# Attention, routing and eight experts in one hand-ordered kernel: the first query copy in two parts, and one more empty place ahead of the transposes of the normed tokens

## The chip, the cores and the metric

The kernel runs on one core of one Trainium2 chip. The metric is device time in microseconds (us); lower is better. The engines are named as in the profile: PE (TensorE; PEld is its weight load), DVE (VectorE), ACT (ScalarE), POOL (GpSimd), and SP (SyncE), which issues most of the DMAs. Times are of the whole program.

## The reference, cut

```python
def attention_block(x, g, b):             # x: 4 batches, 512 tokens, 128 wide
    xn = layernorm(x, g1, b1)             # x itself is normed once before
    q, k, v = xn @ Wq, *split(xn @ Wkv)   # 16 heads of 64 for q; one k and one v for all heads
    attn = softmax(q * 64**-0.5 @ k.T)
    return layernorm((attn @ v) @ Wo, g2, b2)

x = x + attention_block(layernorm(x))
h = layernorm(x)                          # "hn" in the kernel
probs = softmax(h @ gate_w.T)             # 8 experts
topw, sel = top_k(probs, 2); topw /= topw.sum()
for each expert e: out_e = (up * gelu(gate)) @ down_e   # 128 -> 2 x 512 -> 128
x = x + sum over the two chosen experts of topw * out_e
```

Everything is float32.

## The kernel before, in words

**Layout.** The 2048 tokens are four batches of 512; a batch is held as 128 partitions by 4 token tiles of 128. The 16 heads are 8 pairs. The attention works in *steps*: one step is one head pair and one token tile of one batch, so a batch has 32 steps and there are 128. The experts work in 39 tiles of 128 slots: each token's normed row is scattered to two slots in DRAM, sorted by expert, and a tile loads 128 slots of one expert.

**PSUM.** The pool `ps_sc` holds two score tiles of two banks each, `ps_av` one bank for the values' product, and `ps_tp` three banks that everything else takes in turn: transposes, projections, routing, the experts' transposes and down projections. A tile in `ps_tp` has to be copied out before the third one after it may start.

**The attention loop** (`attention`) is an order written out by hand; each engine runs its own instructions in the order in which the program issues them. One turn of the loop takes two steps, i and i+1:

1. `divide` of step i-1 (L330 to L332), then `score` of i and i+1: matmuls L307 on PE, the row maximum `nmax` L314 on DVE.
2. `pieces(PE)`: a place at which other work may put one piece on PE. If there was none, the turn is called `bare`.
3. `turn` of steps i-5 and i-4: 16 transposes L340 of the weights `ex`, and four copies of the results out of PSUM. In a bare turn ACT copies both halves of the first step (L454, L456) and DVE the first half of the second (L452); otherwise DVE copies the second half of the first step (L456) and ACT the rest (L454, L464). Between them `softmax` (L322, exponentials on ACT).
4. `pieces(REST, SOON)`, two rows of values (L350), `divide` of step i, and `pieces(REST, SOON)` again. In the last batch one more `pieces(SOON)`.

**The other work** is a set of Python generators. A `yield` ends a piece and names the kind of place that the next piece waits for: `PE`, `REST` (a plain `yield`) or `SOON`. `advance` gives one place to the first generator in the queue whose kind fits. The list `aheads` holds `project` of the next batch (norm, transposes L255, keys L278, queries L289 with their copy L291, values L297). The list `others` holds, for the batch that has ended, `output` (L374), then `between` (norm, residual, norm again into `hn` with four ACT instructions L216, then a PE place in which `turned` transposes `hn`, L542, and copies it to `hT`, L544), then `route`: gate matmul L576, `logits` L579, the top-2 choice on DVE (L583 to L604), counts `cp` L625 on PE, slot numbers, eight scatters of `hn` on POOL (L652), and `plan`, which tells which expert each tile is of. `between` runs for batches 0, 1 and 2 beside the attention of the next batch.

**The last batch** has no attention after it, so `between_late` and `route` run beside the experts' tiles (3 places in each tile: in the middle of the up projections L820, behind them, and behind the down projections L833). There `hn` is made by DVE (L529), and `hT` is copied by DVE. An expert tile is: transpose `tp_e` L799 of the next tile, its copy `xeT` L801 on ACT, 16 matmuls `gu` L820, `ge` L825 on ACT, `act` L826 on DVE, 8 matmuls `dn` L833, `ye` L838 on DVE, a scatter of the result on POOL (L850). SP loads the tokens `xt` (L779) and the weights (L786, L789) of the tiles ahead.

**The start** (batch 0): `project(0)` runs alone until the keys and the first query tile are there. `wq` is applied to the normed tokens (L289), ACT copies the 512 columns of the result and scales them (L291), and the first turn's scores begin. The score of step (b, p, t) reads only columns t*128 to t*128+127 of `qT[p]`, and all of `kT`.

Of the kernel before, what the change touches and what calls it, by code (L numbers as in the profile page):

```python
# [19 lines left out]
SCALE = DH ** (-0.5)  # L20
# [12 lines left out]
def tile_attention_then_moe(  # L33
# [15 lines left out]
    nc = tc.nc  # L49
    P = 128  # L50
    B, S, D = x.shape
# [132 lines left out]
    def moments(src, tag, twice=False, st=None):  # L184

        n = src.shape[1]
        if st is None:
            st = small.tile([P, n, 6], F32, tag="st", name=f"st_{tag}")  # L190
            for c in range(n):
                nc.vector.bn_stats(st[:, c, :], src[:, c, :])
            yield
        mv = small.tile([P, n, 2], F32, tag="mv", name=f"mv_{tag}")
        for c in range(n):
            nc.vector.bn_aggr(mv[:, c, :], st[:, c, :])
        ve = small.tile([P, n], F32, tag="ve", name=f"ve_{tag}")
        if twice:
            nc.vector.tensor_scalar(ve, mv[:, :, 1], 1.0 + EPS, EPS * EPS, ALU.mult, ALU.add)
        else:  # L200
            nc.vector.tensor_scalar_add(ve, mv[:, :, 1], EPS)
        rstd = small.tile([P, n], F32, tag="rstd", name=f"rstd_{tag}")
        nc.gpsimd.tensor_tensor(rstd, ve, neg_half[:, 0:n], ALU.pow)
        return mv, rstd

    def normalize(dst, src, tag, twice=False):

        mv, rstd = yield from moments(src, tag, twice)
        n = src.shape[1]

        less = small.tile([P, n], F32, tag="less", name=f"less_{tag}")
        nc.gpsimd.tensor_tensor(less, mv[:, :, 0], rstd, ALU.mult)
        nc.gpsimd.tensor_scalar_mul(less, less, -1.0)
        yield
        for c in range(n):
            nc.scalar.activation(  # L216
                dst[:, c, :], src[:, c, :], AF.Identity, bias=less[:, c : c + 1],
                scale=rstd[:, c : c + 1],
            )

    def pause(n):

        for _ in range(n):
            yield
# [19 lines left out]
    def project(b):  # L244


        xn = p2.tile([P, NT, D], F32, tag="ln", name=f"xn_{b}")
        xnT = p1.tile([P, NT, P], F32, tag="xnT", name=f"xnT_{b}")
        xnT_flat = xnT.rearrange("p c t -> p (c t)")
        if b > 0:  # L250
            yield from normalize(xn, xs[b], f"a{b}", twice=True)
            yield PE
            tp = ps_tp.tile([P, NT, P], F32, tag="tp", name=f"tp_x_{b}")
            for c in range(NT):
                nc.tensor.transpose(tp[:, c, :], xn[:, c, :], ident)  # L255
            nc.scalar.activation(xnT, tp, AF.Identity, bias=b1_sb, scale=g1_sb)
        else:

            mv, rstd = yield from moments(xs[b], f"a{b}", True)
            for c in range(NT):  # L260
                nc.vector.tensor_scalar(
                    xn[:, c, :], xs[b][:, c, :], mv[:, c, 0:1], rstd[:, c : c + 1],
                    ALU.subtract, ALU.mult,
                )
            for h in range(2):
                half = slice(h * NT // 2, (h + 1) * NT // 2)
                tp = ps_tp.tile([P, NT // 2, P], F32, tag="tp", name=f"tp_x_{b}_{h}")
                for c in range(NT // 2):
                    nc.tensor.transpose(tp[:, c, :], xn[:, half][:, c, :], ident)
                if h == 0:  # L270
                    nc.vector.tensor_scalar(xnT[:, half], tp, g1_sb, b1_sb, ALU.mult, ALU.add)
                else:
                    nc.scalar.activation(
                        xnT[:, half], tp, AF.Identity, bias=b1_sb, scale=g1_sb
                    )
        yield PE
        kp = ps_tp.tile([P, S], F32, tag="tp", name=f"kp_{b}")
        nc.tensor.matmul(kp, wkk.rearrange("p j d -> p (j d)"), xnT_flat, start=True, stop=True)  # L278
        kT = p2.tile([P, S], F32, tag="kT", name=f"kT_{b}")

        moved = nc.scalar.copy if b > 0 else nc.vector.tensor_copy
        moved(kT, kp)
        v = p2.tile([P, NT, DH], F32, tag="v", name=f"v_{b}")
        qT = []
        if b > 0:
            yield PE
        for c in range(NP):
            qp = ps_tp.tile([P, S], F32, tag="tp", name=f"qp_{b}_{c}")
            nc.tensor.matmul(qp, wq_sb[:, c, :], xnT_flat, start=True, stop=True)  # L289
            qT.append(p9.tile([P, S], F32, tag="qT", name=f"qT_{b}_{c}"))  # L290
            nc.scalar.mul(qT[c], qp, SCALE)  # L291
            qkv[b] = qT, kT, v
            yield PE
            if c == 0:
                vp = ps_tp.tile([P, NT, DH], F32, tag="tp", name=f"vp_{b}")
                for t in range(NT):
                    nc.tensor.matmul(vp[:, t, :], xnT[:, t, :], wv, start=True, stop=True)  # L297
                moved(v, vp)
                yield PE
# [103 lines left out]
    def attention():  # L403
# [10 lines left out]
        held, exTs, oTs, rows, aheads = {}, {}, {}, [], []  # L414
        tiles = experts()
        aheads.append([project(0), REST])
        while 0 not in qkv:
            advance(aheads)
# [11 lines left out]
        for i in range(0, end + TURN, 2):  # L430
            if 0 < i <= end:
                divide(*steps[i - 1], *held[i - 1])
            if i % (NP * NT) == 10 and steps[i][0] + 1 < B:
                b = steps[i][0] + 1
                aheads.append([project(b), REST])
# [55 lines left out]
    def between(g, y):  # L491


        yn = p2.tile([P, NT, D], F32, tag="ln2", name=f"yn_{g}")
        yield from normalize(yn, y, f"c{g}")
        yield
        nc.gpsimd.tensor_tensor(yn, yn, g2_sb.unsqueeze(1).to_broadcast([P, NT, D]), ALU.mult)
        yield
        nc.gpsimd.tensor_tensor(xs[g], xs[g], yn, ALU.add)
        yield  # L500
        hn = p2.tile([P, NT, ROW], F32, tag="hn", name=f"hn_{g}")
        yield from normalize(hn[:, :, 0:D], xs[g], f"d{g}")
        yield PE
        hs[g] = hn, turned(g, hn)
        yield PE

    def between_late(g, y, st):


        mv, rstd = yield from moments(y, f"c{g}", st=st)  # L510
        yield
        xg = xs[g]
        yn = p2.tile([P, NT, D], F32, tag="ln2", name=f"yn_{g}")
        for c in range(NT):
            nc.vector.scalar_tensor_tensor(
                yn[:, c, :], y[:, c, :], mv[:, c, 0:1], g2_sb, ALU.subtract, ALU.mult
            )
        yield
        yield from pause(1)
        for c in range(NT):  # L520
            nc.vector.scalar_tensor_tensor(
                xg[:, c, :], yn[:, c, :], rstd[:, c : c + 1], xg[:, c, :], ALU.mult, ALU.add
            )
        yield
        hn = p2.tile([P, NT, ROW], F32, tag="hn", name=f"hn_{g}")
        mv, rstd = yield from moments(xg, f"d{g}")
        yield from pause(2)
        for c in range(NT):
            nc.vector.tensor_scalar(  # L529
                hn[:, c, 0:D], xg[:, c, :], mv[:, c, 0:1], rstd[:, c : c + 1],  # L530
                ALU.subtract, ALU.mult,
            )
        yield from pause(1)
        yield PE
        hs[g] = hn, turned(g, hn)
        yield from pause(1)
        yield PE

    def turned(g, hn):
        tp = ps_tp.tile([P, NT, P], F32, tag="tp", name=f"tp_h_{g}")  # L540
        for c in range(NT):
            nc.tensor.transpose(tp[:, c, :], hn[:, c, 0:D], ident)  # L542
        hT = p1.tile([P, NT, P], F32, tag="hT", name=f"hT_{g}")
        (nc.vector.tensor_copy if g == B - 1 else nc.scalar.copy)(hT, tp)  # L544
        return hT
# [407 lines left out]
```

## Time and profile before

| | us |
|---|---|
| median of 3 runs | 582.54 (582.27 to 583.16) |
| the profiled execution | 583.46 |
| its span | 581.7 |
| PE busy | 554.7 (95%) |
| DVE busy | 383.3 (66%) |
| ACT busy | 358.7 (62%) |
| POOL busy | 335.1 (58%) |
| PE's mean granted clock | 0.987 |

The profile shows one execution; its span runs from the first to the last instruction, and the profiled execution's own time is 1.76 us longer. In a timeline line the columns are: start, duration, engine, line of the kernel, instruction, output <- input, the shapes, how many instructions are drawn together (x4), and in brackets the time for which the engine stood idle before it and what ended that. Durations of a group that was drawn together run from the first start to the last end. In the list of waits each row gives the waiting engine and line, the releasing engine and line, the total in us, how often, and the longest. A few matmul records can be missing, so a group may show fewer than were issued.

The attention of batches 0 to 2 fills about 14 to 405 us, that of batch 3 ends at 452, and the experts' tiles fill 458 to 562. In the attention one turn of the loop takes 5.71 us without extra PE work.

### The profile page before, as it was taken

How to read it: one execution, taken by the hardware profiler on the slowest of the kernel's cores; microseconds unless marked ns; L12 is line 12 of the kernel's file. 1: busy time of each engine (PE TensorE's matmuls, PEld its weight loads, DVE VectorE, ACT ScalarE, POOL GpSimd, SP SyncE). 2: the span in 40 equal slices, each digit the busy share in tenths (PEclk: the TensorE clock that was granted, in tenths of full speed). 3: DMA queues.
4: the chain of work that ended last, by engine and by line, in shares of the span. 5: the costliest groups of instructions: out<-in, count | busy, mean ns of one | idle time of the engine just before them, and what ended most of it. 6: DMA issues, size and time to landing. Idle time of an engine off the chain costs nothing.

```text
span 581.7 us, 10509 instructions
## 1 busy us (share of the span) xinstructions
PE 554.7 (95%) x3391; PEld 346.2 (60%) x3391; DVE 383.3 (66%) x949; ACT 358.7 (62%) x912; POOL 335.1 (58%) x354
## 2 busy tenths in 40 slices
PE   7899999999999999999999999999999999999980
PEld 5354455545655545566455546654554999999970
DVE  3767666667668688666677877567795378444433
ACT  2779767776678767867887776678865322222210
POOL 3756554456557568755665787457678045743340
PEclk9999999999999999999999999999999999999995
DMA  8990000000000000200000005000000179999945
GB/s 242 300 279 2 1 1 1 1 1 2 1 1 1 0 2 26 73 5 2 0 1 2 10 22 186 4 2 2 0 7 32 47 231 298 350 339 314 320 139 217
DMA packets 38729, 50.33 MB, mean 87 GB/s; under 512 B 4356, under 2 KB 27142, under 8 KB 38673
## 3 DMA queue, kind: packets, MB, share of 16 engines
q1 hardware_dynamic: 35232, 43.44, 24.2%
q0 software_dynamic: 2144, 4.46, 2.1%
q10 hardware_dynamic: 1296, 1.74, 0.8%
q8 instruction: 28, 0.46, 0.3%
q14 instruction: 29, 0.23, 0.1%
HBM read 37.11 MB, written 15.29 MB: 90 GB/s over the span
## 4 chain that ended last, share of the span: by engine, by line
PE 74%; DVE 6%; issue 5%; ACT 5%; DMA 4%; POOL 4%; SPq 0%; POOLq 0%; DVEq 0%; ACTq 0%
PE av L350 18%; PE sc L307 18%; PE tp L340 18%; PE yp L374 5%; PE qp L289 5%; PE gu L820 4%; DMA parts<-ye,row 3%; ACT ex L322 3%; POOL parts L850 3%; DVE nmax L314 2%; PE dn L833 2%; DMA yy<-parts 1%; PE warm L128 1%; DVE ex L332 1%; PE kp L278 1%
## 5 line engine op out<-in xcount | busy, mean ns | idle before, releaser
L331 POOL TENSOR_SCALAR ex<-ex,rden 128x512 f32<-128x512 f32 x128 | 220.2, 1723 | 143.6 <-DVE rden L330 135.4
L322 ACT ACTIVATE ex<-sc,nmax 128x512 f32<-128x512 f32 x256 | 175.8, 707 | 5.9 <-DVE nmax L314 5.9
L314 DVE TENSOR_REDUCE nmax<-sc 128x2 f32<-128x1024 f32 x128 | 150.1, 1213 | 2.0 <-PE sc L307 2.0
L340 PEld LDWEIGHTS tp<-ident,ex 128*128 128x128 f32 x1024 | 112.9, 141 | 34.8 <-issue 20.9
L307 PE MATMUL sc<-kT,qT 64*128 64x512 f32 x512 | 128.4, 617 | 4.2 <-ACT ex L322 3.5
L340 PE MATMUL tp<-ident,ex 128*128 128x128 f32 x1024 | 128.0, 275 | 0.7 <-ACT exT L454 0.3
L350 PE MATMUL av<-exT,v 128*64 128x512 f32 x512 | 124.9, 605 | 0.2 <-ACT exT L454 0.2
L307 PEld LDWEIGHTS sc<-kT,qT 64*128 64x128 f32 x512 | 43.4, 185 | 87.7 <-ACT ex L322 41.9
L454 ACT COPY exT<-tp 128x512 f32<-128x512 f32 x113 | 66.8, 591 | 19.4 <-PE tp L340 19.2
L330 DVE RECIPROCAL rden<-den 128x2 f32<-128x2 f32 x128 | 21.0, 164 | 83.2 <-ACT ex L322 79.6
L332 DVE TENSOR_SCALAR ex<-ex,rden 128x512 f32<-128x512 f32 x128 | 69.6, 543 | 4.5
L820 PE MATMUL gu<-xeT,gu 128*128 128x128 f32 x560 | 71.1, 281 | 0.0
L825 ACT ACTIVATE ge<-gu 128x512 f32<-128x512 f32 x35 | 20.9, 597 | 73.3 <-PE gu L820 71.0
L820 PEld LDWEIGHTS gu<-xeT,gu 128*128 128x128 f32 x560 | 65.1, 192 | 1.0
L850 POOL DMA_INDIRECT parts<-ye,row x35 | 34.4, 982 | 50.3 <-DVE ye L838 39.9
L350 PEld LDWEIGHTS av<-exT,v 128*64 128x64 f32 x512 | 32.9, 136 | 47.4 <-issue 45.5
L322 ACT ACTIVATION_READ_ACCUMULATOR ex<-sc,nmax 128x1 f32 x256 | 57.0, 223 | 0.0
L826 DVE TENSOR_TENSOR act<-ge,gu 128x512 f32<-128x512 f32 x35 | 24.0, 687 | 41.1 <-ACT ge L825 39.4
L456 DVE COPY exT<-tp 128x512 f32<-128x512 f32 x48 | 33.1, 690 | 26.1 <-PE tp L340 25.8
L291 ACT ACTIVATE qT<-qp 128x512 f32<-128x512 f32 x32 | 19.0, 601 | 38.7 <-PE qp L289 38.7
L464 ACT COPY exT<-tp 128x512 f32<-128x512 f32 x64 | 39.6, 619 | 0.6 <-PE tp L340 0.6
L652 POOL DMA_INDIRECT slots<-hn,index x32 | 33.1, 1036 | 10.9 <-PE tp_e L799 5.9
(160 smaller groups left out, 468.9 us busy)
## 6 DMA issues: line engine op xcount, KB each, us to landing
gu<-in_gate_up_t_dram SPq DMA_DIRECT2D x38, 512.0 KB
down<-in_down_t_dram SPq DMA_DIRECT2D x38, 256.0 KB
slots<-blank SPq DMA_DIRECT2D x26, 360.0 KB
xt<-slots SPq DMA_DIRECT2D x38, 72.0 KB
yy<-parts SPq DMA_DIRECT2D x4, 512.0 KB
out_dram<-x ACTq DMA_DIRECT2D x4, 256.0 KB
x<-in_x_dram SPq DMA_DIRECT2D x3, 256.0 KB
parts<-ye,row POOLq DMA_INDIRECT x35, 4.9
```

The costliest lines, as they stand in the source:

```text
L307: nc.tensor.matmul(sc[:, j, :], qT[p][half, t * P : (t + 1) * P], kT[half, :], start=True, stop=True)
L314: nc.vector.tensor_reduce(nmax, sc, AX.X, ALU.max, negate=True)
L322: nc.scalar.activation(ex[:, j, :], sc[:, j, :], AF.Exp, bias=nmax[:, j : j + 1], accum_out=den[:, j : j + 1],)
L331: nc.gpsimd.tensor_scalar_mul(ex[:, 0, :], ex[:, 0, :], rden[:, 0:1])
L332: nc.vector.tensor_scalar_mul(ex[:, 1, :], ex[:, 1, :], rden[:, 1:2])
L340: nc.tensor.transpose(tp[:, c, :], ex[:, j, c * P : (c + 1) * P], ident)
L350: nc.tensor.matmul(av[j * DH : (j + 1) * DH, :], v[:, c, :], exT[:, j, c, :], start=(c == 0), stop=(c == NT - 1),)
L454: nc.scalar.copy(*copies[0])
L456: (nc.scalar.copy if bare else nc.vector.tensor_copy)(*copies[1])
L464: nc.scalar.copy(*copies[1])
L820: latest[:] = [nc.tensor.matmul(ps[:, j, g, :], gu[:, at : at + P], xT, start=True, stop=True)]
L850: apart(added, nc.gpsimd.indirect_dma_start(parts, bass.IndirectOffsetOnAxis(ap=row[:, c : c + 1], axis=0), y[:, c, :], None, bounds_check ...
```

## The change

Three edits:

- `project`: the very first copy of a query tile (batch 0, head pair 0) is made by two ACT instructions, columns 0 to 127 and columns 128 to 511, instead of one.
- `between` (batches 0, 1, 2): one more plain `yield` behind the norm and ahead of the PE place. `turned`, and all of `route` behind it, come one turn of the loop later.
- `between_late` (batch 3): `pause(2)` instead of `pause(1)` ahead of the PE place: one more of the experts' places is left empty.

```diff
@@ project
             qT.append(p9.tile([P, S], F32, tag="qT", name=f"qT_{b}_{c}"))
-            nc.scalar.mul(qT[c], qp, SCALE)
+
+            for some_of in ([slice(0, P), slice(P, S)] if b == c == 0 else [slice(0, S)]):
+                nc.scalar.mul(qT[c][:, some_of], qp[:, some_of], SCALE)
             qkv[b] = qT, kT, v
             yield PE
@@ between
         hn = p2.tile([P, NT, ROW], F32, tag="hn", name=f"hn_{g}")
         yield from normalize(hn[:, :, 0:D], xs[g], f"d{g}")
+        yield
         yield PE
         hs[g] = hn, turned(g, hn)
         yield PE
@@ between_late
                 ALU.subtract, ALU.mult,
             )
-        yield from pause(1)
+        yield from pause(2)
         yield PE
         hs[g] = hn, turned(g, hn)
         yield from pause(1)
         yield PE
```

How the instructions move on the engines, as the two programs stand: ACT has one instruction more. In batches 0 and 1 `tp_h` and `hT`, and `lp`, `cp` and their ACT and DVE work, stand one turn later. In batch 2, whose turns have no projection of a next batch beside them, the turn that held `tp_h` becomes a bare one and the turn after it does not: ACT and DVE change places in two copies of each. In the last batch `tp_h` stands behind `tp_e` of tile 4 and the down projections of tile 2, instead of ahead of them, and `hT` on DVE behind `ye` of tile 2; the order of SP's instructions is the same.

## The prediction

> **What bounds the kernel now.** I read the page's rows of busy time and of 40 slices first, then the chain of work that ended last, then PE's waits, then the timeline around each edited line.
>
> ```profile
> PE 554.7 (95%) x3391; PEld 346.2 (60%) x3391; DVE 383.3 (66%) x949; ACT 358.7 (62%) x912; POOL 335.1 (58%) x354
> ...
> PE   7899999999999999999999999999999999999980
> ```
>
> TensorE (PE) is busy for 554.7 of 581.7 us, and in every slice but the first two and the last two it is full; the chain of waits gives PE 74% of the span. So an edit counts only where it shortens PE's instructions or ends one of its waits (27 us in all, most of them in the first and last slices). PE's waits by line (columns: total us, times, longest us):
>
> ```profile
> PE sc L307 <- ACT ex L322: 3.5, 7, 0.7
> ...
> PE tp_h L542 <- DVE hn L529: 0.7, 1, 0.7
> PE sc L307 <- ACT qT L291: 0.7, 1, 0.7
> ...
> PE tp_h L542 <- ACT hn L216: 0.5, 1, 0.5
> ...
> PE dn L833 <- ACT xeT L801: 0.4, 1, 0.4
> ```
>
> Three of these belong to the edited lines: the first score waits for qT (0.7), and tp_h, the transposes of the normed tokens, for hn (0.7 late, 0.5 between batches). They show only whole waits; a tp_h whose four transposes each start as their quarter of hn appears is counted as busy while it crawls, so I compare durations too. Four transposes cost 0.43 us where nothing is late: tp_x starts at 162.47 and the next matmul at 162.90 (the loop's sixteen, 410.16 to the values at 412.09, would give 0.48).
>
> **Step 1, the first query copy in two (start).**
>
> ```profile
> 10.75 0.60 ACT L291 ACTIVATE qT<-qp 128x512 f32<-128x512 f32 x1 [2.07 <-PE qp L289]
> 11.40 1.99 PE L307 MATMUL sc<-kT,qT 64*128 64x512 f32 x8 [0.69 <-ACT qT L291]
> ```
>
> The copy ends at 11.35 and the score starts 0.05 later. kT was there at 10.58 (9.89 + 0.69), so qT alone sets the start. ACT's copies from PSUM take 0.265 us for 128 columns (y_at L378), 0.372 for 256 (L298), 0.60 for 512. So the first part ends at 10.75 + 0.27 = 11.02, and the first score starts at about 11.07: 0.33 earlier. The second part, 384 columns, lies between 0.372 and 0.60, I take 0.48, and ends at about 11.50; the second score, which alone needs it, comes 1.0 after the first, at 12.07. Its cover is 0.57. From there the chain nmax, ex, transposes shifts along with PE; wq had landed by 7.99. Bounds: 0 (nmax or a later wait eats it) to 0.60. I take 0.33. The Trainium skill, "VectorE: DVE Perf Modes", section "The TRN2 errata", speaks against cutting: each ScalarE instruction pays a fixed part (172 cycles plus the columns at 1.2 GHz from PSUM), so two parts would cost 0.71 us where one costs 0.57, an estimate; the row of 0.60 agrees with it. By it the first part is still 0.32 earlier, since only that part is waited for.
>
> **Step 2, one more empty place in between().** It moves tp_h, its copy hT, and all of the routing behind it (lp, logits, the top-2 chain on DVE, cp, index, the scatters issued by POOL, and the plan that SP's xt loads read) one turn of the attention loop later, for batches 0, 1 and 2. Instruction counts do not change. SP's order does not change; POOL's scatters come some 6 to 7 us later, and the first xt load that needs those of batch 2 is issued at 479.9, while POOL could start them near 451, so nothing waits for them.
>
> Batches 0 and 1: tp_h runs right behind the scores, and hn has only just started:
>
> ```profile
> 187.83 1.68 ACT L216 ACTIVATE hn<-x,less_d,rstd_d 128x128 f32<-128x128 f32 x4
> ...
> 189.04 0.86 PE L542 MATMUL tp_h<-ident,hn 128*128 128x128 f32 x4
> ```
>
> Score to score this turn takes 7.28 (187.12 to 194.40); a turn with a query projection and no tp_h takes 6.68. So tp_h costs 0.60 against 0.43 when hn is ready. One turn later it is ready: 0.16 each, twice. lp (+0.90) and cp (+0.45) also shift by a turn at the same cost. Bounds: -0.3 each (DVE's part of the route falls before a copy L456 that leaves only 0.15 us before the values L350 need it; the smaller waits of PE for exT are 0.2 to 0.3) to +0.17.
>
> Batch 2 is worse, as ACT has no slack there:
>
> ```profile
> 408.29 1.65 ACT L216 ACTIVATE hn<-x,less_d,rstd_d 128x128 f32<-128x128 f32 x4 [0.67 <-POOL less_d L213]
> 408.84 1.48 PE L542 MATMUL tp_h<-ident,hn 128*128 128x128 f32 x4 [0.52 <-ACT hn L216]
> ```
>
> This turn takes 8.09 (405.86 to 413.95) against 5.71 + 0.43 = 6.14: 1.95 lost. Of it 0.55 lies in the scores ahead (waiting for ex) and stays. After the change no projection piece is left for this turn, so the loop takes its "bare" branch: ACT copies the first tile's second half (L456), DVE the second tile's first. The transposes of the weights start at about 408.4, but their first copy stands on ACT behind hn, which ends at 409.94; the third PSUM bank of three is then used up, and I find the fourth group of transposes some 0.8 late. Turn: 5.71 + 0.55 + 0.8 = 7.07; then 6.15 with a clean tp_h, then 6.60 with lp. 8.09 + 6.60 + 5.71 = 20.40 becomes 7.07 + 6.15 + 6.60 = 19.82: **0.58**. Bounds: 0 (ACT as late as now: its 7.00 us of work in the 8.09 are more than a bare turn holds, and only hT's 0.59 leaves it) to 1.4 (no stall of the copies at all).
>
> **Step 3, one more place in between_late.** Experts give places three times a tile: amid the up projections, behind them, behind the down ones. Now tp_h stands ahead of tp_e(4) and dn(2):
>
> ```profile
> 469.44 1.12 DVE L529 TENSOR_SCALAR hn<-x,mv_d,rstd_d 128x128 f32<-128x128 f32 x4 [0.41 <-issue]
> 469.93 1.01 PE L542 MATMUL tp_h<-ident,hn 128*128 128x128 f32 x4 [0.71 <-DVE hn L529]
> 470.78 0.27 PE L799 MATMUL tp_e<-ident,xt 128*128 128x128 f32 x1
> ...
> 481.18 1.16 PE L833 MATMUL dn<-down,act 128*128 128x128 f32 x8 [0.41 <-ACT xeT L801]
> ```
>
> PE's up projections end at 469.06, tp_e(4) starts at 470.78: 1.72 for a 0.43 job. After, tp_e(4) goes at 469.06, dn(2) at 469.17 to 470.07, and tp_h from 470.07 with three quarters of hn ready (one each 0.28 from 469.44, the last at 470.56); it ends at about 470.8, where up(4) starts, instead of 471.78: **1.0**. hT stands on DVE behind ye(2) and of(4), until about 472.4; lp needs it at 472.67. The route behind it and its eight scatters on POOL come one place (about 1 us) later, between the scatters of the experts' results. SP's load of tile 17's tokens, the first to need them, is issued at 504.02; the last scatter starts at 497.25 and lands 5.1 later by the page of that stretch, 502.35, so 1.7 us are left and the move takes one of them. dn(5) later waited 0.60 (weights) for xeT(7), because it had tp_e(7)'s bank of the three; with tp_h moved it takes another bank and waits, by my count, for ye(4): 0.15. So 0.35 more, in all 1.35. Bounds: 0.3 (hT late for lp by its own 0.68, dn as now) to 1.5.
>
> **Sum.** 0.33 + 0.32 + 0.58 + 1.35 = 2.58. The profiled execution took 583.46 (span 581.7 and 1.76 around it), so 580.9 by its own time; it lies 0.92 above the median of the runs shown (582.54), from which I get 579.96: **580.0 us**. The ends of the four steps would give -0.3 to 3.8; all four at one end is unlikely.
>
> **Rivals.** (A) A wait takes tp_h's place between batches: ACT's copies behind hn in batch 2 and DVE's route pieces ahead of L456 in 0 and 1. For it: ACT is busy 7.00 of 8.09 us there, and 6.41 stay for a turn whose PE work is 5.71. Against it: the next turns had ACT at 4.89 of 6.60 and 4.05 of 5.71, so the backlog has somewhere to go. Gain 0.33 + 1.35 = 1.7: 580.9. (B) The late gain is given back: hT, now behind DVE's expert work, is late for lp, and dn(5) meets another holder of its bank. For it: the margin is only 0.25. Against: DVE is idle between. Gain 0.33 + 0.32 + 0.58 + 0.3 = 1.5: 581.0. Both at once: 581.9, no difference. (C) The split gives nothing, the fixed cost of the second part delaying the second score and the 1.2 us nmax that follow it: 580.3. For it only the cover of 0.57 us being wrong. (D) Slower: DVE's route pieces, a turn later, stand in front of nmax, so ex is late and scores wait as in the row of 3.5 us (7 times, 0.5 each). Four pieces in each of three batches are 12 places; at 0.5 each 6.0 against the 2.6: 585.9. It decides from 0.31 each (12 x 0.31 = 2.6 + 1.2). For it: DVE is busy 5.36, 5.33 and 5.93 us of 6.60, 5.71 and 6.44 in the turns behind 413.95. Against: the same pieces stand in the same sort of turn now, where 0.28 is the most I find lost.
>
> **Chances.** Forecast 0.55 (579.3 to 581.0), A 0.15, B 0.10, A and B 0.05, C 0.05, D 0.10. A change under 0.2% (1.17 us) can't be told from none: faster means below 581.4, slower above 583.7. Faster: 0.55, two thirds of A, 0.6 of B, and C: 0.76; same 0.14; slower 0.10. The range takes A, B and both, and a sum larger by 1.2 at the upper ends of batch 2 and the start: 578.8 to 582.6.
>
> **What would show it.** Right: first score near 11.07 in a profile with the same start; tp_h x4 in 0.43 to 0.45 three times between batches and without a wait; the turn of batch 2 near 7.1, then 6.15; no wait of tp_h beside the experts, up(4) about a microsecond earlier after the same up(3); dn waiting under 0.2. Wrong: a new row "PE tp L340 <- ACT exT" over 0.8, "PE av L350" waits that recur, "PE lp L576 <- DVE hT", more than 7 waits of scores for ex, or tile 17's load waiting for the scatters of the last batch.

## The result and the profile after

| us | before | after |
|---|---|---|
| median (5 runs each) | 582.54 (582.27 to 583.24) | 579.83 (579.41 to 580.56) |
| the profiled execution, its span | 583.46, 581.7 | 579.79, 578.1 |
| start of the output projection of batch 3, from the first query projection | 442.54 | 441.52 |
| start of tp_e of tile 8, from the first query projection (the *mark*) | 474.28 | 471.50 |
| start of the last tp_e, from the first query projection | 549.56 | 546.78 |
| from there to the end of the span | 22.45 | 21.64 |

The ratio is 0.9954 with a 95% interval of 0.9943 to 0.9964: **faster by 2.7 us**. The mark, counted from the start of the first query projection (9.69 before, 9.68 after), moves by 2.78, and from there on the two traces run in step; I use it below, as it repeats to 0.1 us from run to run. The other 0.8 of the spans' 3.6 is the tail of that one execution of before: another profile of the same kernel (e11) has a mark of 474.27 and a tail of 21.80.

Lines of the changed kernel stand two or three higher: L309 was L307, L342 L340, L352 L350, L456 L454, L545 L542, L836 L833. The row of busy time of the page after:

```profile
PE 553.4 (96%) x3391; PEld 346.1 (60%) x3391; DVE 384.5 (67%) x949; ACT 358.6 (62%) x913; POOL 334.4 (58%) x354
```

PE is busy for 1.3 us less at the same number of instructions: these are mostly transposes that crept along behind hn and now run at full pace (tp_h in batch 2: 1.48 before, 0.66 after). Its list of waits (columns as before: total, times, longest):

```profile
PE sc L309 <- ACT ex L324: 3.5, 7, 0.7
...
PE tp L342 <- ACT exT L456: 0.9, 2, 0.7
...
PE dn L836 <- DVE act L829: 0.5, 1, 0.5
PE sc L309 <- ACT qT L293: 0.4, 1, 0.4
```

Both rows of tp_h and the row of dn waiting for xeT are gone, the wait for qT fell from 0.7 to 0.4, and one new wait has come: 0.7 of the loop's transposes for a copy on ACT. The scores' waits for ex are as they were, 3.5 in 7.

The start, in the timeline after:

```profile
10.74 0.66 ACT L293 ACTIVATE qT<-qp 128x128 f32<-128x128 f32 x2 [2.08 <-PE qp L289]
11.07 1.99 PE L309 MATMUL sc<-kT,qT 64*128 64x512 f32 x8 [0.37 <-ACT qT L293]
```

The two parts are drawn together (x2, under the first one's shape) and end at 11.40; all eight score matmuls still run in 1.99, so the second score waits for nothing.

The two turns of batch 2, in the timeline after:

```profile
407.56 1.65 ACT L216 ACTIVATE hn<-x,less_d,rstd_d 128x128 f32<-128x128 f32 x4 [0.68 <-POOL less_d L213]
...
409.13 0.56 ACT L456 COPY exT<-tp 128x512 f32<-128x512 f32 x1
...
409.74 0.66 PE L342 MATMUL tp<-ident,ex 128*128 128x128 f32 x4 [0.68 <-ACT exT L456]
...
414.11 0.66 PE L545 MATMUL tp_h<-ident,hn 128*128 128x128 f32 x4
...
416.54 2.23 PE L352 MATMUL av<-exT,v 128*64 128x512 f32 x8
```

The first turn takes 7.06 (405.13 to 412.19) instead of 8.09. In it the fourth group of transposes stands for a bank that ACT empties only behind hn. The next one, with a clean tp_h, takes 6.51, and its values take 2.23 where 1.94 is usual.

And beside the experts:

```profile
468.06 1.31 DVE L532 TENSOR_SCALAR hn<-x,mv_d,rstd_d 128x128 f32<-128x128 f32 x4
...
469.03 0.72 PE L545 MATMUL tp_h<-ident,hn 128*128 128x128 f32 x4
...
469.59 1.96 PE L823 MATMUL gu<-xeT,gu 128*128 128x128 f32 x16
...
478.43 1.13 PE L836 MATMUL dn<-down,act 128*128 128x128 f32 x8
```

tp_h runs without a wait, 1.0 behind the start of hn instead of 0.49, and dn of tile 5 (the last line) has lost the 0.41 that it waited.

### The profile page after: what moved, and what is told of

It reads as the page before. It is cut to its first block, busy times and chain, and to the rows that moved or that the text cites. A ratio compares the mean times of both kernels' runs of the same rounds, so it can differ in the third digit from the quotient of the medians.

```text
span 578.1 us, 10508 instructions
## 1 busy us (share of the span) xinstructions
PE 553.4 (96%) x3391; PEld 346.1 (60%) x3391; DVE 384.5 (67%) x949; ACT 358.6 (62%) x913; POOL 334.4 (58%) x354
## 3 DMA queue, kind: packets, MB, share of 16 engines
q10 hardware_dynamic: 1296, 1.74, 0.8%
## 4 chain that ended last, share of the span: by engine, by line
PE 78%; issue 5%; ACT 5%; DMA 4%; POOL 4%; DVE 2%; SPq 0%; POOLq 0%; DVEq 0%; ACTq 0%
PE av L352 19%; PE sc L309 19%; PE tp L342 18%; PE yp L376 5%; PE gu L823 5%; PE qp L289 5%; DMA parts<-ye,row 3%; ACT ex L324 3%; POOL parts L853 3%; PE dn L836 2%; DMA yy<-parts 1%; DVE nmax L316 1%; PE warm L128 1%; PE kp L278 1%; ACT exT L456 1%
## 5 line engine op out<-in xcount | busy, mean ns | idle before, releaser
L342 PEld LDWEIGHTS tp<-ident,ex 128*128 128x128 f32 x1024 | 112.9, 141 | 35.6 <-issue 18.3
L309 PE MATMUL sc<-kT,qT 64*128 64x512 f32 x512 | 128.5, 617 | 3.9 <-ACT ex L324 3.5
L342 PE MATMUL tp<-ident,ex 128*128 128x128 f32 x1024 | 128.2, 276 | 1.4 <-ACT exT L456 0.9
L352 PE MATMUL av<-exT,v 128*64 128x512 f32 x512 | 125.1, 605 | 0.2 <-ACT exT L456 0.2
L309 PEld LDWEIGHTS sc<-kT,qT 64*128 64x128 f32 x512 | 43.5, 185 | 87.4 <-ACT ex L324 42.8
L456 ACT COPY exT<-tp 128x512 f32<-128x512 f32 x113 | 66.8, 591 | 17.3 <-PE tp L342 17.0
L352 PEld LDWEIGHTS av<-exT,v 128*64 128x64 f32 x512 | 32.9, 136 | 47.5 <-issue 45.8
L293 ACT ACTIVATE qT<-qp 128x512 f32<-128x512 f32 (+2 forms) x33 | 19.0, 587 | 35.1 <-PE qp L289 35.1
```

The costliest lines, as they stand in the source:

```text
L309: nc.tensor.matmul(sc[:, j, :], qT[p][half, t * P : (t + 1) * P], kT[half, :], start=True, stop=True)
L342: nc.tensor.transpose(tp[:, c, :], ex[:, j, c * P : (c + 1) * P], ident)
L352: nc.tensor.matmul(av[j * DH : (j + 1) * DH, :], v[:, c, :], exT[:, j, c, :], start=(c == 0), stop=(c == NT - 1),)
L456: nc.scalar.copy(*copies[0])
```

## The experiments

All marks are of tp_e of tile 8 unless said. e1 to e4 ran on one chip and e5 to e8 on another; on both the kernel before took 590.52 (median): in the traces of e1 to e8 PE stands for 1.5 to 4.6 us at one tile's up projections, near 500 us and behind tile 10. The mark lies ahead of that. e9 to e12 ran where the kernel before took 582.4 to 582.5.

| kernel | mark | median, us | before beside it |
|---|---|---|---|
| e1 split alone | 473.96 | 590.29 | 590.52 |
| e2 between() alone | 473.40 | 588.72 | 590.52 |
| e3 late pause alone | 472.70 | 586.39 | 590.52 |
| e4 change without batch 2 | 472.00 | 587.33 | 590.52 |
| e5 change, hn of batch 2 two and two | 470.75 | 585.70 | 590.52 |
| e6 change, late pause 3 | 472.30 | 587.32 | 590.52 |
| e7 change, two turns later | 472.47 | 588.70 | 590.52 |
| e8 the change again | 471.57 | 586.25 | 590.52 |
| e9 change, first projection in two | 471.19 | 579.27 | 582.43 |
| e10 as e5, copies swapped | 470.37 | 578.67 | 582.43 |
| e11 before again | 474.27 | 582.75 | 582.43 |
| e12 e9 and e10 together | 470.02 | 578.53 | 582.50 |

**e1, e2, e3: each edit alone.** Each holds just its own hunk of the diff.

> Only the first query copy in two parts. As a mark I use the start of the last tp_e of the experts (559.25 in the profile before, 556.46 after), since the tail behind it varies from run to run by more than a step is worth. Theory (the first score waits for its 128 columns alone, and everything behind shifts along): first score at 11.07 instead of 11.40, mark at 558.92, time 0.33 below before, too small for the times to tell. Rival 1 (a later wait eats the gain): first score at 11.07, mark at 559.25. Rival 2 (the second part makes the second score late): scores in two pieces, mark 559.1 or later.

> Only the extra place in between() for batches 0, 1 and 2. Theory (steps are independent; in the trace after they are worth 0.20 + 0.20 + 0.30): mark at 558.55, time 0.7 below before. Rival (the experts gain by this too, since the extra place changes the order of tp_e of tiles 0 and 1 against the last batch's output projection, and with it the PSUM banks behind): the 0.60 wait of dn of tile 5 goes as well, mark at 557.95.

> Only the longer pause in between_late. Theory (tp_h waited for hn, and dn of tile 5 waited for the bank of tp_e of tile 7 because of where tp_h took its bank): 1.16 + 0.60, mark at 557.49, time 1.76 below before, dn of tile 5 without a wait. Rival (the 0.60 is owed to the edit in between(), which changes the order of tp_e and the output projection): 1.16 alone, mark at 558.09, and the wait of dn for xeT stays.

Measured against 474.28: 0.32, 0.88 and 1.58. They add up to 2.78, which is what the change as a whole moves. e1 went as the theory said, to 0.01, and its second score was not late; its last-tp_e mark is useless here, since the stall near 500 us comes before it. In e2 batches 0 and 1 gave 0.40 and batch 2 0.32 up to the output projection (441.82 there); 0.17 more came beside the experts, though the wait of dn for xeT stayed: DVE begins hn 0.03 after the end of the up projections of tile 3 instead of 0.38, so tp_h waits 0.36 instead of 0.71. Its rival fell. The 0.35 is an idle of 0.41 that DVE has right ahead of hn, waiting for nothing that the profile names: it is there in before, e1, e3, e4 and e11, which lack the move of batch 2, and gone in after, e2, e5, e6, e8, e9, e10 and e12, which have it. So that move takes it away; how is not shown. In e3 the 0.60 of dn went with the late pause alone, so the rival that gave it to between() fell too; 1.58 instead of 1.76, as the 0.17 of e2 is not there. From the end of the up projections of tile 3 to the start of those of tile 4, e3 takes 1.73 (2.72 before, 1.56 in the change as a whole):

```profile
468.99 0.27 PE L799 MATMUL tp_e<-ident,xt 128*128 128x128 f32 x1
...
470.00 0.89 PE L542 MATMUL tp_h<-ident,hn 128*128 128x128 f32 x4
470.72 1.96 PE L820 MATMUL gu<-xeT,gu 128*128 128x128 f32 x16
```

**e4: batches 0 and 1 only.** In between():

```diff
-        yield
+        if g < 2:
+            yield
```

> The changed kernel, but the extra place in between() only for batches 0 and 1. Theory (the move in batch 2 is worth the 0.30 that the trace shows up to the output projection): mark at 556.76, time 0.3 above after; the turn of batch 2 takes 8.09 again. Rival 1 (worth 0.58, as forecast, the rest being lost elsewhere by chance): mark at 557.04. Rival 2 (worth nothing, since ACT is full beside batch 3 wherever tp_h stands): mark at 556.46.

The mark is 0.50 above after: batch 2's move is worth 0.30 in the attention (the theory) and 0.2 beside the experts. The turn took 8.09 again.

**e5: hn of batch 2 two and two.** In normalize():

```diff
         for c in range(n):
+            if tag == "d2" and c == n // 2:
+                yield
```

> The changed kernel, but in batch 2 the four ACT instructions that make hn are issued two and two, the second two behind the copies and exponentials of the next turn; tp_h stays where it is. As marks I use the turns of the attention loop, and the start of tp_e of tile 8 counted from the start of the first query projection (474.28 before, 471.50 after). Theory (in the turn that lost its tp_h the fourth group of transposes waits 0.68 for a PSUM bank, because the first copy stands on ACT behind hn's 1.65): the turn of 7.06 becomes 6.3 to 6.5, the wait PE tp <- ACT exT falls to 0.3 (the one that was there before), mark at 470.8 to 471.0. Rival (ACT has no room in these turns; what is not lost there is lost one turn later): the turn of 7.06 gets shorter, but the next one of 6.51 longer by the same, mark at 471.4 to 471.6.

The timeline of PE in e5, transposes and values of the two turns:

```profile
407.35 2.09 PE L344 MATMUL tp<-ident,ex 128*128 128x128 f32 x16
...
415.58 2.25 PE L354 MATMUL av<-exT,v 128*64 128x512 f32 x8
```

All 16 transposes run in one go, the turn takes 6.28, the mark falls by 0.75 to 470.75. So the 0.68 was hn's place on ACT, as the theory said, and was not lost again behind. But the next turn still took 6.52, its values 2.25: its surplus is not ACT's backlog from the turn before.

**e10: that surplus.** On top of e5:

```diff
-            bare = not early and not pieces(PE)
+            bare = not early and (not pieces(PE) or i == 120)
```

> The kernel with hn of batch 2 made two and two, and besides the turn that holds tp_h of batch 2 made to share its copies as a bare turn does (DVE takes the first half of the second step, ACT the second half of the first). That turn takes 6.5 us, 0.4 more than a clean tp_h should cost. Theory (hT's 0.59 stands on ACT ahead of the copies, so the values wait about 0.3 for the last of ACT's copies, L456 of the second step): the turn becomes 6.1 to 6.3, mark (tp_e of tile 8 from the first query projection) 470.3 to 470.5 instead of 470.75. Rival (ACT has one copy more ahead of the exponentials then, and they are late for the next scores): 6.5 or more, or the same again lost in the turn behind.

The copies and the values of that turn in e10:

```profile
413.61 0.59 ACT L549 COPY hT<-tp_h 128x512 f32<-128x512 f32 x1 [0.23 <-PE tp_h L547]
414.09 0.59 ACT L458 COPY exT<-tp 128x512 f32<-128x512 f32 x1
414.57 0.60 ACT L460 COPY exT<-tp 128x512 f32<-128x512 f32 x1
415.00 0.69 DVE L456 COPY exT<-tp 128x512 f32<-128x512 f32 x1
...
415.33 1.94 PE L354 MATMUL av<-exT,v 128*64 128x512 f32 x8
```

The values take 1.94 again and the turn 6.20; the mark is 0.38 below e5, as forecast, and the exponentials were not late. But the theory's reason does not hold. The values of this turn read both copies of its first step. In the change ACT has made the first of them by 415.88, though hT's 0.59 stands ahead of it, and the values start at 416.54. The second is DVE's, and it comes right behind the row maxima:

```profile
413.85 2.33 DVE L316 TENSOR_REDUCE nmax<-sc 128x2 f32<-128x1024 f32 x2
...
416.11 0.67 DVE L458 COPY exT<-tp 128x512 f32<-128x512 f32 x1
```

It ends at 416.78, and the second matmul of the values, which reads it, starts at 416.84, 0.30 behind the first (0.01 behind it in e10). No list of waits shows this, as the first matmul still runs. In e10 that copy is ACT's (L460, done at 415.17). So the surplus was DVE's copy behind the row maxima, and giving it to ACT ended it.

**e6, e7: later still.** `pause(3)` in between_late, and three empty places instead of one in between() (which is two turns later than before).

> The changed kernel with one more place of pause in between_late (3 instead of 2). Theory (one place was enough to have hn ready; what counts beyond is which PSUM banks the tiles behind get, and here dn of tile 5 gets none that is still being copied): mark (tp_e of tile 8 from the first query projection) at 471.5 as after, within 0.1, though tp_h, lp and cp stand one place later. Rival (the later the better, as DVE gets more time for hT): mark 0.2 or more below 471.5.

> The changed kernel with tp_h and the route of batches 0, 1 and 2 two turns later than before instead of one. Theory: batches 0 and 1 gain nothing more (tp_h costs 0.40 clean already); in batch 2 the 0.68 stall stays in the turn behind hn, and the turns behind it shift; beside the experts the order of the small tiles turns out so that dn of tile 6 takes the PSUM bank of tp_e of tile 8, as dn of tile 5 took that of tile 7 before the change: a wait of 0.4 (0.6 for the weights) for xeT comes back, a tile later. Mark taken at tp_e of tile 10, by then all is behind: 480.08 before, 477.29 after, 477.9 here less what batch 2 gains (0 to 0.36). Rival (the 0.60 of the late gain came from the place of tp_h and not from the banks): no wait of dn for xeT, 477.3 or less.

Both missed. In e6 dn of tile 5 did not wait, as said, but the mark is 0.8 worse than after (rival: better). One tile later the counts ask DVE for a sum that isn't there:

```profile
479.53 0.58 PE L628 MATMUL cp<-some,below 128*128 128x8 f32 x4 [0.41 <-DVE some L601]
```

PE reached it 0.4 early, and stood for it: later is not better, each step behind tp_h has its own margin. In e7 batches 0 and 1 gained nothing more, and dn of tile 6 waits for xeT as foretold:

```profile
482.63 1.16 PE L838 MATMUL dn<-down,act 128*128 128x128 f32 x8 [0.41 <-ACT xeT L806]
```

so that wait goes with the bank that dn is given. But at tile 10 the mark is 478.86, a microsecond above the forecast: the last batch's hn slipped as well (DVE waited 1.32 for rstd from POOL), tp_h waited 0.37 for it and dn of tile 3 0.24 for ye. In batch 2, tp_h fell into the other sort of turn, whose values read copies of the turn before: with hT in the same place on ACT that turn took 6.21 instead of 6.51.

**e8, e11: the two kernels again.**

> The changed kernel as it is. On the chip of the first four experiments the kernel before took 590.5 instead of 582.5, and one tile's up projection stood about 2.5 to 2.9 us for its weights near 500 us. Theory (the gain lies ahead of that stretch): tp_e of tile 8 at 471.50 from the first query projection on any chip, and the time 2.7 below before where weights come in time. Rival (where weights come late, a PE that is ahead only waits longer for them): the mark is the same but the gain in time is below 1.5.

> The kernel before as it is, for the trace of it on a chip where it takes 590 us. Theory (what makes it 8 us longer there is one stretch near 500 us in which the weights of one tile come late, PE's clock falls and SP's loads stand still; the change does not touch it): tp_e of tile 8 at 474.28 as before, and 6.5 to 8 us lost between tile 10 and the last, against 5.4 to 7.5 in the experiments so far. Rival (the change takes part in it, as the whole stretch starts earlier or later): tile 10 to the last differs from that of the changed kernel (76.05 there) by more than the experiments differ among themselves (74.9 to 77.0).

The marks repeat (471.57 and 474.27). On its chip e8 gained 4.27 (ratio 0.9928, 0.9904 to 0.9952, which is 2.8 to 5.7 us): its rival fell, and the theory's 2.7 lies just outside. e11 came to the other chip, where tile 10 to the last takes 69.49 before and after alike; what the stall near 500 us costs the kernel before where e8 ran is therefore not known, and stays open.

**e9: the first projection in two as well.**

```diff
-            nc.tensor.matmul(qp, wq_sb[:, c, :], xnT_flat, start=True, stop=True)
...
+            halves = [(qp, slice(0, S))]
+            if b == c == 0:
+                qp0 = ps_av.tile([P, S], F32, tag="av", name="qp_first")
+                halves = [(qp0, slice(0, P)), (qp, slice(P, S))]
+            for to, some_of in halves:
+                nc.tensor.matmul(
+                    to[:, some_of], wq_sb[:, c, :], xnT_flat[:, some_of], start=True, stop=True
+                )
+            for to, some_of in halves:
+                nc.scalar.mul(qT[c][:, some_of], to[:, some_of], SCALE)
```

> The changed kernel, but the first query projection too is made in two matmuls, the first for the 128 columns that the first score reads, in a PSUM bank of its own (that of the values' product, which is free then). Theory (after the change the first score waits 0.37 for qT, because ACT cannot start until all 512 columns are projected, 1.06 after the projection starts): the first part of qT is done 0.6 after the start of the projection, kT 0.88 after it, so PE itself (projection done at 1.02) sets the start: first score 1.05 after the start of the projection, against 1.39 after the change and 1.71 before; tp_e of tile 8 at 471.2 instead of 471.5. Rival (what is gained ahead of the first score is lost to nmax and the exponentials, whose first wait DVE and ACT set): first score earlier, but the mark at 471.5.

The start in e9:

```profile
9.68 0.38 PE L296 MATMUL qp_first<-xnT,wq_sb 128*128 128x128 f32 x2
...
10.10 0.28 ACT L300 ACTIVATE qT<-qp_first 128x128 f32<-128x128 f32 x1 [1.44 <-PE qp_first L296]
10.72 1.99 PE L316 MATMUL sc<-kT,qT 64*128 64x512 f32 x8
10.75 0.49 ACT L300 ACTIVATE qT<-qp 128x384 f32<-128x384 f32 x1 [0.37 <-PE qp L296]
```

The first score starts 1.04 after the projection, with no wait. The mark is 0.31 lower, as forecast.

**e12: e9 and e10 together.**

> All that gained, together: the change, hn of batch 2 two and two, the copies of the tp_h turn shared as in a bare turn, and the first query projection in two matmuls. Theory (the steps lie on PE's path one behind the other and add): first score 1.05 after the start of the first query projection, turns of batch 2 at 6.3 and 6.2, tp_e of tile 8 at 470.06 (470.37 with the two edits of batch 2, less 0.31), against 471.50 after the change and 474.28 before; time 4.2 below before, 1.4 below after. Rival (the sum is less, a later wait takes part of it): mark at 470.3 or more.

The mark is 470.02, the sum of the parts. 578.53 is the shortest median of all: ratio 0.9933 to before, 0.9919 to 0.9946; 1.3 below the change's own median.

## Why the prediction was right, step by step

The forecast was 580.0 with a sum of 2.58; the time is 579.83, the mark moved by 2.78.

- **Step 1, right in mechanism and size:** 0.33 forecast, 0.32 in e1. The second part took 0.49 (0.48 forecast). Cutting does cost: 0.28 and 0.49, as e9 shows the parts apart, are 0.77 for 0.60. This agrees with the fixed cost per instruction of the Trainium skill ("VectorE: DVE Perf Modes", "The TRN2 errata"), from which the estimate was 0.71 for 0.57. It fell on ACT under cover of the first score. Rival C fell.
- **Step 2, batches 0 and 1:** 0.40 for 0.32. A clean tp_h adds 0.40 to a turn (7.08 against 6.68), not 0.43. The bound of -0.3, and rival D with it, did not come true: the scores' waits for ex stayed at 3.5 in 7.
- **Step 2, batch 2:** 0.30 for 0.58 in the attention. The first turn came out at 7.06 (7.07 forecast), and its stall at 0.68 (0.8). The term that failed is "then 6.15 with a clean tp_h": the turn took 6.51, because I counted tp_h's time on PE alone. In this turn, which is not bare, the values also need DVE's copy, which ended at 416.78 and held them by 0.30 (e10). It is the narrow margin of a DVE copy that I had named as a bound for batches 0 and 1 (0.15), but not here. The part of rival A that held, ACT behind hn, was in the sum already. My sign of a wrong forecast, a row of over 0.8 for tp waiting for ACT, came up (0.9), but 0.3 of that was there before, and the stall itself had been counted: a badly set mark.
- **Step 3, right in mechanism, too small in size:** by itself (e3) 1.58 for 1.35. The stall at tp_h gave what was forecast, 0.99 for 1.0: up(4) started 1.73 behind the end of up(3), for 1.74. The term that was mis-sized is dn of tile 5: it lost all its 0.60, and the 0.15 that I left for ye of tile 4 was not there. Rival B fell: hT was done at 471.05, lp started at 471.38 without a wait.
- **What no term had:** step 2 helps step 3. With the move of batch 2, hn began as the up projections ended (468.06 for 468.03), 0.35 earlier against PE than before, and up(4) followed up(3) 0.17 sooner (1.56) than in e3. I had added the steps as if each stood alone. That DVE's idle of 0.41 would go is not in the prediction, and its cause stays open.
- The errors, -0.01, +0.08, -0.28 and +0.23, and the 0.18 beside the experts (e4) that no term had, partly cancel: the sum came out 0.20 short. That it came so close is in part luck.

## What to carry to other kernels

The row of 0.5 for tp_h in batch 2 stood for 1.35 us, 0.52 of waiting and 0.83 of creeping (408.84 to 410.16 against 414.11 to 414.60 after): look for groups that take longer than the same instructions elsewhere, and for later waits (here for a PSUM bank) that come from the same order. Moving a step later on the bound engine pays only until its input is ready; past that, every step behind it moves into margins of its own (e6 and e7 lost 0.8 and more). When a step moves, ask of each copy that PE reads next which engine makes it, and what that engine does just before: DVE's copy behind the row maxima cost 0.3 in a turn where tp_h on PE was clean. And a gain of the forecast size does not prove its reason (e10): look for the operand that came last.

## What the runs showed of the hardware

**The clock falls after a short idle.** In e3, PE stood 2.48 us near 500 us, up to 503.84. The stretches behind it (columns: length, then busy us and instructions of PE, PEld, DVE, ACT and POOL, the granted clock, the DMA share, GB/s):

```profile
504.00:505.00 1.00, 1.00 (x10) 1.00 (x11) 0.00 (x0) 0.00 (x0) 0.82 (x1) 1.00 0.40 148
505.00:506.00 1.00, 1.00 (x7) 1.00 (x7) 0.00 (x0) 0.00 (x0) 0.77 (x3) 0.55 0.20 70
506.00:507.00 1.00, 1.00 (x7) 1.00 (x6) 0.00 (x0) 0.00 (x0) 0.51 (x2) 0.50 0.00 0
507.00:508.00 1.00, 1.00 (x6) 1.00 (x6) 0.23 (x1) 0.07 (x1) 0.00 (x0) 0.50 0.20 66
508.00:509.00 1.00, 0.69 (x4) 0.40 (x4) 0.50 (x2) 0.68 (x2) 0.66 (x1) 0.74 0.20 61
```

PE ran at full clock again for about one microsecond, and only then at half for about 3.4 (by the clock's column), with 6 or 7 matmuls in a microsecond instead of 10. A wait of 2.5 us thus cost up to 1.7 more, an estimate from these rows (half of 3.4). The Trainium skill ("TensorE: Matmul & The Clock Gate", "HAM oscillation") tells of half clock behind idle gaps of over about 3.4 us; the half agrees with the rows, but here a gap of 2.48 was enough (2.89 in e1). The length alone does not decide: in e8 PE stood 2.41 and then ran at a clock of 1.00 from 503 to 506; the clock fell to 0.50 only behind a second gap, of 1.85. What does decide, no run here shows.

Nor does any run show what held PE near 500 us. That one tile's weights came late, as the expectations of e8 and e11 have it, is not shown: the profile names no releaser, ACT and DVE stood too (3.80 and 3.19 us in e3), and PE went on 0.05 behind ACT's copy xeT.
